# A four-level Perceiver on one core: the experts of levels 1 to 3 by one code on gathered tokens

## The chip, the cores and the metric

The kernel runs on one core of a Trainium2 chip. Its time is what the device measures for one execution, in microseconds (us); for the kernel before it is the median of three runs. The core has five engines with instruction streams of their own: TensorE (PE in the profile, PEld for its weight loads), VectorE (DVE), ScalarE (ACT), GpSimd (POOL) and SyncE (SP), which here only starts transfers. All arithmetic is float32; TensorE carries out each float32 matmul of the program as two instructions, so counts in the profile are twice those in the code.

## The reference, cut to what matters

A state x of 2 x 64 tokens (128 rows) with 256 features goes through four levels. Each level adds a cross-attention on a context (2 x 1024 x 192), a mixing stage, and a mixture of eight experts, each applied to the layer norm of x:

```python
x = x + _L1_attn_ref(_layernorm(x), L1_attn_W, L1_attn_b)
x = x + _L1_ffn_ref(_layernorm(x), L1_ffn_gate_w, L1_ffn_w1, L1_ffn_b1, L1_ffn_w2, L1_ffn_b2)
...
# _L1_ffn_ref                                   # 256 -> 1024 -> 256
logits = xf @ gate_w
top_w, top_idx = jax.lax.top_k(logits, 2)
top_w = jax.nn.softmax(top_w, axis=-1)
combine = jnp.zeros((t, 8)).at[jnp.arange(t)[:, None], top_idx].add(top_w)
h = jax.nn.gelu(jnp.einsum('td,edf->tef', xf, w1) + b1, approximate=False)
y = jnp.einsum('tef,efd->ted', h, w2) + b2
out = jnp.einsum('ted,te->td', y, combine)
# _L2_ffn_ref                                   # 256 -> 512 -> 256, no biases
h = jax.nn.silu(jnp.einsum('nd,ehd->neh', xf, w_gate)) * jnp.einsum('nd,ehd->neh', xf, w_up)
# _L3_ffn_ref                                   # 256 -> 1024 -> 256
gate_logits = x @ Wg + bg
h = jnp.einsum('td,edh->eth', xf, W0) + b0[:, None, :]
g = jax.nn.silu(jnp.einsum('td,edh->eth', xf, W1) + b1[:, None, :])
y = jnp.einsum('eth,ehd->etd', h * g, W2) + b2[:, None, :]
```

Each token uses its two best of the eight experts, so a quarter of all token-expert pairs counts. From the reference's routers, the tokens per expert are, for the inputs used: level 1: 57, 0, 41, 9, 7, 19, 51, 72; level 2: 34, 5, 16, 41, 1, 75, 42, 42; level 3: 0, 3, 26, 58, 109, 0, 54, 6.

## The kernel before, in words

The 128 tokens lie on the 128 partitions. The stages are called by level and place: l0x, l0a, l0f, l1x, l1a (a dynamic convolution), l1f, l2x, l2t (a test-time-trained layer with a Newton-Schulz iteration), l2f, l3x, l3a (a scan), l3f. In every stage TensorE multiplies, and ScalarE or VectorE takes the sums out of PSUM.

**Dense experts (l0f, l1f, l2f).** All 128 tokens go through all eight experts, one expert after the other, and the routing weight (zero for most) scales what comes out. `features` (L354) computes 128 hidden features at a time, with the weights as the stationary operand; `Mix.add` (L345) multiplies the hidden features by the second weights and adds the result, times the expert's column of `comb`, to x on VectorE (L349). `gate` (L301) is the router: it multiplies the transposed layer norm of x by the router's weights and finds the two best experts on VectorE. `expert_bias` (L328) adds l1f's second biases. `later` (L293) delays each expert's second matmuls behind the next expert's first. The first biases of l1f are added by ScalarE in its gelu (L1176), one activation for each 128 features.

**Gathered experts (l3f, from L1800).** A matmul with a triangle (`upto`, L1857) numbers the tokens of each expert; `to_slot` (L1865) is a one-hot matrix from tokens to 64 slots for each expert. A round r handles experts 2r and 2r+1 side by side, 64 columns each. `gather` (L1871) multiplies by the one-hot matrix, `hidden` (L1886) makes the hidden features with the tokens as stationary operand (64 columns) and the weights moving (512 wide), `turn` (L1905) transposes them, `out_of` (L1918) multiplies by the second weights, `scatter` (L1928) brings the rows back to their tokens and adds them to `acc` in PSUM. The bias sums start each PSUM bank by a matmul of one-hot rows (`biases`, L1822). After four rounds comes a fifth, OVER, of four blocks of 32 slots for experts with more than 64 tokens. Which experts these are is known only at run time: a chain on VectorE (L1948 to L1994) writes indices, and GpSimd fetches the blocks' weights by indirect transfers (L2011), twelve of 1 MB or as halves; a block that is not used has an index out of bounds, and nothing is moved for it.

**Buffers.** Weights go through a pool with three rings: w8 (six tiles of 1 MB), w4 (four tiles of 512 KB) and w2 (six of 256 KB). l3f has six more tiles of 1 MB (`more_w`). SyncE issues all other weight loads, in an order that a scheduler chose; each waits until the last reader of its buffer's previous content is done. `weight` (L124, transfer at L131) asks for a tile and starts its load.

**Order.** A scheduler orders the instructions of each engine, except in blocks under `in_written_order` (L268), where TensorE, VectorE, ScalarE and GpSimd keep the order of the code. Some work of later stages is written into earlier ones as filler (`steps`, L440): keys and values of l3x (L374 to L405) run in l1a, around l1f's end and around l2f.

`layernorm` (L225) takes statistics on VectorE, a square root on ScalarE with the activation table of the next function loaded behind it (`rstd_of`, L216), and a reciprocal; `transposed` (L240) transposes by TensorE and copies the result out of PSUM.

Of the kernel before, what the change touches and what calls it, by code (L numbers as in the profile page):

```python
# [17 lines left out]
P = 128  # L18
# [39 lines left out]
def tile_perceiver(ctx: ExitStack, tc: tile.TileContext, i: dict, out: bass.AP):  # L58
# [79 lines left out]
    routers = const.tile([P, 2, N_SMALL], F32, name="routers")  # L138
    ctx_gb = const.tile([CH, 4], F32, name="ctx_gb")
# [188 lines left out]
    def expert_bias(x, comb, b2):  # L328

        ps = bank()  # L330
        nc.tensor.transpose(ps[0:8, :P], comb, ident)
        cT = tok.tile([8, P], F32, tag="cT", name="cT")
        nc.vector.tensor_copy(cT, ps[0:8, :P])
        ps = bank()
        nc.tensor.matmul(ps[:, :D], cT, b2, start=True, stop=True)
        return residual(x, ps[:, :D])


# [101 lines left out]
    def steps(work, n=9):  # L440

        for _, _ in zip(range(n), work):
            pass

# [370 lines left out]
    steps(fill[0], 3)  # L815
    with psum(2, 4), stage_pool(name="l0a", bufs=1) as pool, in_written_order():
# [297 lines left out]


    with psum(2, 4), stage_pool(name="l1a", bufs=1) as pool, in_written_order():
# [24 lines left out]
        for k in range(6):  # L1141
# [8 lines left out]
            for r, dst in places:  # L1150
# [6 lines left out]
                )  # L1157
        bandT = transposed(band, 1, pool, "bandT", "bandT")
# [606 lines left out]
    with psum(2, 3), stage_pool(name="l3a", bufs=1) as pool:  # L1765
# [34 lines left out]
        x = residual(x, ps[:, :D])  # L1800

    with psum(2, 3), stage_pool(name="l3f", bufs=1) as pool, stage_pool(
# [230 lines left out]
        for r in range(OVER + 1):  # L2039
# [26 lines left out]
            if r:  # L2066
                out_of(r - 1, last_w2)
# [172 lines left out]
```

## Time and profile before

| what | us |
|---|---|
| median of three runs (741.34 to 745.24) | 742.32 |
| the profiled execution | 739.35 |
| its span, first to last instruction | 737.6 |
| TensorE busy | 673.0 |
| l1f: x of l1a done to x of l1f done | 211.04 to 277.69 |
| l2f: x of l2t done to x of l2f done | 536.34 to 583.18 |
| l3f: x of l3a done to x of l3f done | 646.88 to 734.80 |

The mean granted TensorE clock of the profiled execution is 0.972. In the profile, a line of the timeline gives a start, a length, the engine, the line of the code, the operation, what it writes and reads, the shapes and how many instructions stand together; brackets give idle time ahead of it and what ended it. The groups of instructions give busy time, then mean length in ns, then idle time ahead.

### The profile page before, as it was taken

Reading aid. Unit: us, or ns where it says so; the run is one execution under the profiler, and the core shown is the slowest. Engines: PE = TensorE matmul, PEld = TensorE weight load, DVE = VectorE, ACT = ScalarE, POOL = GpSimd, SP = SyncE. Lnnn points to the kernel's source line nnn. Section 1 sums busy time; section 2 is a strip of 40 time slices with the busy share of each in tenths; the row PEclk is TensorE's granted clock in tenths of the full one; section 3 lists DMA queues with packets and bytes.
Section 4 is the critical chain, followed back from the end, with each engine's and each line's share of the span. In section 5 each row is a group of like instructions: output and inputs, shape, how many; then the busy total and the mean of one; then the engine's idle time right before and its main releaser. Section 6 shows DMA issues by size and latency. Waiting matters only on the chain.

```text
span 737.6 us, 11286 instructions
## 1 busy us (share of the span) xinstructions
PE 673.0 (91%) x4624; PEld 497.3 (67%) x4624; DVE 284.7 (39%) x718; ACT 268.2 (36%) x542; POOL 66.6 (9%) x92
## 2 busy tenths in 40 slices
PE   7779979989879999999999989999999989679987
PEld 4446658856659996766767678999889756534434
DVE  5853443267440003343342344534232267451111
ACT  2352343278533333323333425306130388322111
POOL 3530100000100000000000030210000000000240
PEclk9999999999969999999999999999999999979999
DMA  9930013830006887000000400030158700628951
GB/s 292 422 141 1 15 36 119 304 120 2 1 1 232 289 294 270 1 0 1 1 1 9 163 1 1 1 109 7 59 199 289 254 0 2 267 94 347 419 192 73
DMA packets 19302, 92.76 MB, mean 126 GB/s; under 512 B 3298, under 2 KB 5876, under 8 KB 10068
## 3 DMA queue, kind: packets, MB, share of 16 engines
q1 hardware_dynamic: 16976, 85.70, 31.5%
q0 software_dynamic: 2016, 6.30, 2.3%
q8 instruction: 36, 0.59, 0.3%
q14 instruction: 14, 0.11, 0.0%
q10 hardware_dynamic: 260, 0.06, 0.0%
HBM read 98.20 MB, written 0.13 MB: 133 GB/s over the span
## 4 chain that ended last, share of the span: by engine, by line
PE 76%; DVE 8%; issue 7%; ACT 6%; DMA 2%; POOL 1%; POOLq 0%; DVEq 0%; ACTq 0%
PE bank L255 34%; PE two_banks L1245 4%; PE bank L988 4%; PE bank L247 3%; PE two_banks L959 3%; PE two_banks L1250 2%; PE bank L1014 2%; PE two_banks L1417 2%; PE two_banks L1896 2%; PE two_banks L374 2%; PE bank L1537 2%; PE two_banks L400 1%; ACT pT L997 1%; PE two_banks L255 1%; PE bank L1525 1%
## 5 line engine op out<-in xcount | busy, mean ns | idle before, releaser
L255 PEld LDWEIGHTS bank<-l2x_ctx,pT 128*128 128x128 f32 x256 | 42.2, 190 | 7.9 <-ACT pT L104 4.9
L255 PE MATMUL bank<-l2x_ctx,pT 128*128 128x192 f32 x256 | 44.4, 327 | 0.6 <-ACT pT L104 0.6
L349 DVE SCALAR_TENSOR_TENSOR x_new<-bank,comb,x_new 128x256 f32<-128x256 f32 x24 | 11.6, 483 | 80.0 <-PE bank L255 80.0
L988 PEld LDWEIGHTS bank<-ident,p 128*128 128x128 f32 x256 | 29.6, 149 | 17.3 <-issue 6.1
L988 PE MATMUL bank<-ident,p 128*128 128x128 f32 x256 | 39.4, 297 | 1.2 <-ACT pT L997 0.5
L967 DVE TENSOR_REDUCE negmax<-two_banks 128x1 f32<-128x1024 f32 x32 | 37.6, 1215 | 5.8 <-PE two_banks L959 5.8
L973 ACT ACTIVATE p<-two_banks,negmax 128x1024 f32<-128x1024 f32 x32 | 36.1, 1127 | 0.8 <-DVE negmax L967 0.8
L1245 PE MATMUL two_banks<-ctxA,l2x_qA 128*128 128x512 f32 x64 | 32.6, 597 | 0.5 <-DVE l2x_qA L102 0.5
L255 PEld LDWEIGHTS bank<-xT,l1f_w_sb 128*128 128x128 f32 x256 | 31.9, 204 | 0.6 <-issue 0.3
L255 PE MATMUL bank<-xT,l1f_w_sb 128*128 128x128 f32 x256 | 32.2, 287 | 0.0
L997 ACT COPY pT<-bank 128x512 f32<-128x512 f32 x48 | 26.9, 588 | 14.5 <-PE bank L988 14.5
L1176 ACT ACTIVATE l1f_hT<-bank,cols 128x128 f32<-128x128 f32 x64 | 18.3, 369 | 35.0 <-PE bank L255 35.0
L255 PEld LDWEIGHTS bank<-xT,l2f_w_sb 128*128 128x128 f32 x256 | 29.6, 192 | 0.3
L255 PE MATMUL bank<-xT,l2f_w_sb 128*128 128x128 f32 x256 | 29.8, 275 | 0.0
L104 ACT COPY pT<-bank 128x512 f32<-128x512 f32 (+1 forms) x22 | 12.1, 557 | 47.8 <-PE bank L247 47.8
L255 PE MATMUL bank<-l1f_w_sb,l1f_hT 128*128 128x256 f32 x128 | 28.8, 379 | 0.0
L1255 DVE TENSOR_REDUCE negmax<-two_banks 128x1 f32<-128x1024 f32 x16 | 19.6, 1224 | 20.8 <-PE two_banks L1250 20.8
L247 PEld LDWEIGHTS bank<-ident,p 128*128 128x128 f32 x164 | 17.7, 141 | 13.8 <-issue 11.8
L959 PE MATMUL two_banks<-n_kT,n_qx 32*128 32x512 f32 x128 | 23.8, 641 | 2.8 <-ACT n_kT L435 1.8
L255 PEld LDWEIGHTS bank<-l1f_w_sb,l1f_hT 128*128 128x128 f32 x128 | 23.8, 190 | 2.9
L262 POOL TENSOR_TENSOR x_bias<-x_new,rows 128x256 f32<-128x256 f32 x4 | 2.9, 726 | 240.7 <-DVE x_new L349 236.2
L247 PE MATMUL bank<-ident,p 128*128 128x128 f32 x164 | 22.6, 279 | 0.7 <-DVE pT L102 0.6
(552 smaller groups left out, 1318.9 us busy)
## 6 DMA issues: line engine op xcount, KB each, us to landing
l1f_w_sb<-in_l1f_w_dram SPq DMA_DIRECT2D x16, 1024.0 KB, 4.8
l3f_w_sb<-in_l3f_w_dram SPq DMA_DIRECT2D x12, 1024.0 KB, 5.1
more_w<-in_l3f_w_dram SPq DMA_DIRECT2D x12, 1024.0 KB, 9.7
l0f_w_sb<-in_l0f_w_dram SPq DMA_DIRECT2D x8, 1024.0 KB, 8.1
l2f_w_sb<-in_l2f_w_dram SPq DMA_DIRECT2D x8, 1024.0 KB, 4.7
l2f_w_sb<-in_l2f_w_dram SPq DMA_DIRECT2D x8, 512.0 KB, 4.6
xh<-in_ctx_dram SPq DMA_DIRECT2D x8, 192.0 KB, 5.2
l2x_ctx<-in_ctx_dram SPq DMA_DIRECT2D x1, 1536.0 KB
```

The lines of the kernel that those rows point to most:

```text
L247: nc.tensor.transpose(ps[:, c * P : (c + 1) * P], src[:, (at + c) * P : (at + c + 1) * P], ident)
L255: nc.tensor.matmul(dst, lhsT, rhs, start=(k == 0), stop=(k == len(pairs) - 1))
L374: nc.tensor.matmul(dst[n], ctxA[:, b, n, keys], w[:, 0, :], start=True, stop=False)
L959: nc.tensor.matmul(sc[u][:, n * 512 : (n + 1) * 512], qx[rows_, c, n, b].rearrange("p h q -> p (h q)"), kT[c, b][rows_, n, :], start=True, ...
L967: nc.vector.tensor_reduce(sc[u][1], sc[u][0], AX.X, ALU.max, negate=True)
L973: nc.scalar.activation(p[u], sc[u][0], AF.Exp, bias=sc[u][1], scale=1.0, accum_out=total[u // 4][:, u % 4 : u % 4 + 1],)
L988: nc.tensor.transpose(ps[:, kc * P : (kc + 1) * P], p[u][:, (4 * k + kc) * P : (4 * k + kc + 1) * P], ident,)
L997: nc.scalar.copy(dst, ps)
L1014: nc.tensor.matmul(po[32 * t : 32 * t + 32, :P], v[:, b, kc // 4, kc % 4, c * P + 32 * t : c * P + 32 * t + 32], pT[4 * g + t, k][:, kc % ...
L1176: nc.scalar.activation(hT[:, at + f, :], ps[:, f * P : (f + 1) * P], AF.Gelu, bias=col("l1f_b1", e * 8 + at + f), scale=1.0,)
L1245: nc.tensor.matmul(dst[n], qA[:, j, b].rearrange("p h q -> p (h q)"), ctxA[:, b, n, :], start=True, stop=False,)
L1255: nc.vector.tensor_reduce(negmax, sc, AX.X, ALU.max, negate=True)
```

## The change

l1f and l2f take the gathered form that l3f has, and all three call one function, `experts`. What a stage gives it: the kind ("gelu": one hidden matrix with bias; "gated": two halves of 512 columns, no bias; "both": two matrices with biases), its constants (`Counting`), where each weight tile lies (`Shelf`, with a function `place`), and the order in which GpSimd fetches the overflow's weights (`blocks`). l0f stays dense.

- **Router.** It reads the transpose of x itself. Since the layer norm is (x - mean) times rstd, the logits are (x W - mean * column sums of W) * rstd. The negative column sums, `less_sums`, are made once ahead of l0a by two matmuls with ones. In l1f and l2f rstd goes into the scale of the tanh; in l3f, with its bias, into one more VectorE operation. The layer norm is still computed, for the gather.
- **First biases.** `sums_of` writes the bias sums of round 0 in the stage in front: in l1a ahead of the transpose of the band, in l3a ahead of its last transposes.
- **Order inside a round.** The overflow's plan comes after round 0 on VectorE; `ways_back` (transposes of slot_w and comb, second biases) moved from round 0 to round 1.
- **Buffers.** l1f has four further 1 MB tiles. In l2f the second weights use w4 tiles, and in the overflow blocks 2 and 3 use halves in w2 tiles, each cleared by GpSimd ahead of its transfer. In l3f the overflow's order is now: first matrix of all blocks, second matrix (halves in w4 tiles for blocks 0 and 1), then the last matrix of blocks 2, 3, 0, 1. In the code n numbers a stage's matrices (1 and 0 give hidden features, 2 the output) and j the expert in a round, or the block of the overflow: n0 of j2 is block 2's second hidden matrix.
- **Else.** The l1f bias columns leave the constants; l1a, l1f and l2f use one PSUM bank fewer for single tiles.

The built program also differs, by the scheduler's choice, in l2x (both context matmuls of an iteration stand ahead of the weighing; before, one stood on either side), in some of l2t's order, and in where l3f's first bias matmuls stand: behind l3x's last matmuls, ahead of l3a's first transposes.

New functions, cut to what the prediction speaks of:

```python
class Shelf:
    def load(self, r):                    # by SyncE
        for n in self.order:
...
            for j in range(2):
                t = self.room(self.place(r, j, n), chunks * wide)
                nc.sync.dma_start(t, src[2 * r + j].rearrange("p c f -> p (c f)"))
...
    def fetch(self, blocks, index, index2):   # by GpSimd
        for j, n in blocks:
...
            tag = self.place(OVER, j, n)
            parts = 2 if tag == "halves" else 1
            for k in range(parts):
                size = chunks * wide // parts
                t = self.room(tag if parts == 1 else "w4" if size > 512 else "w2", size)
                if size == 512:
                    nc.gpsimd.memset(t, 0.0)
                at = index[:, j : j + 1] if parts == 1 else index2[:, j, k : k + 1]
                nc.gpsimd.indirect_dma_start(
...

def experts(name, kind, x, consts, shelf, blocks, pool, acc, bias=None, b2=None, fill=(), sums=None):
...
    steps(fill, 1)
    ps = bank()
    for c in range(2):
        nc.tensor.transpose(ps[:, c * P : (c + 1) * P], x[:, c * P : (c + 1) * P], ident)
    xT = tok.tile([P, 2, P], F32, tag="xT", name="xT")
    nc.scalar.copy(xT.rearrange("p c t -> p (c t)"), ps[:, :D])
    st, mv = stat(6, "bn_st"), stat(2, "bn_mv")
    nc.vector.bn_stats(st, x)
    nc.vector.bn_aggr(mv, st)
    r_ = rstd_of(mv[:, 1:2], 1, table)
    xl = tok.tile([P, D], F32, tag="xl", name="xl")
    nc.vector.tensor_scalar(xl, x, mv[:, 0:1], r_, ALU.subtract, ALU.mult)
    ps = bank()
    accumulate(ps[:, :8], [(xT[:, c, :], router(name, c)) for c in range(2)])
    steps(fill, 2)
...
    for r in range(OVER + 1):
        if r == OVER:
            sums = sums_of(kind, consts, own_over)
        elif r or sums is None:
            sums = sums_of(kind, consts, None if kind == "gated" else consts.of_pair[r])
        prod = hidden(r, sums)
        if r == 0:
            shelf.load(2)
            shelf.load(3)
        if kind != "gated":
            turn(r, prod, 0)
        if r:
            out_of(r - 1)
        if r < OVER:
            gather(r + 1)
        turn(r, prod, 0 if kind == "gated" else 1)
        if r == 0:
            plan_blocks()
        if r == 1:
            ways_back()
        if r:
            scatter(r - 1)
    out_of(OVER)
    scatter(OVER)
    return residual(x, acc)
```

The stages' own part of the diff, cut:

```diff
@@ -813,6 +1170,10 @@
     kv1.room(ahead1.enter_context(stage_pool(name="l1x_k", bufs=1)), pieces)
     fill = [kv1.keys(0, 0), kv1.keys(0, 1), kv1.keys(1, 0), kv1.values(1, 2)]
     steps(fill[0], 3)
+
+    ps = bank()
+    accumulate(ps[:, :N_SMALL], [(ones, routers[:, c, :]) for c in range(2)])
+    nc.scalar.mul(less_sums, ps[:, :N_SMALL], -1.0)
...
-
-    with psum(2, 4), stage_pool(name="l1a", bufs=1) as pool, in_written_order():
+    def place1(r, j, n):
+        if r == OVER:
+            return "more" if n == 1 else "w8"
+        return "more" if (r, n) in ((1, 2), (2, 1)) else "w8"
+
+    beside = ExitStack()
+    shelf = Shelf(
+        "l1f", (1, 2), place1, beside.enter_context(stage_pool(name="l1f_more", bufs=4))
+    )
...
@@ -1155,6 +1530,7 @@
                     dst, src[r, PAD - far : PAD - far + width], bits[r, k : k + 1], dst,
                     ALU.mult, ALU.add,
                 )
+        sums = sums_of("gelu", consts, consts.of_pair[0])
...
@@ -1163,25 +1539,15 @@
         steps(fill[2])
 
 
-    with psum(2, 4), stage_pool(name="l1f", bufs=2) as pool:
-        xlT = transposed(layernorm(x, then=AF.Gelu), 2)
-        mix = Mix(x, gate(xlT, "l1f"))
-        for e in range(8):
-            w1 = weight("l1f_w1", e)
-            w2 = weight("l1f_w2", e)
-            hT = pool.tile([P, 8, P], F32, name="l1f_hT")
-            for at in (0, 4):
-                ps = features(xlT, w1, at, 4)
-                for f in range(4):
-                    nc.scalar.activation(
-                        hT[:, at + f, :], ps[:, f * P : (f + 1) * P], AF.Gelu,
-                        bias=col("l1f_b1", e * 8 + at + f), scale=1.0,
-                    )
-            if e == 0:
-                mix.x = expert_bias(mix.x, mix.comb, l1f_b2)
-            later(lambda hT=hT, w2=w2, e=e: mix.add(hT, w2, e))
-        later()
-        x = mix.x
+    with psum(2, 3), stage_pool(name="l1f", bufs=1) as pool, stage_pool(
+        name="ps_acc", bufs=1, space=PSUM
+    ) as acc_pool, in_written_order():
+        x = experts(
+            "l1f", "gelu", x, consts, shelf,
+            [(j, n) for n in (1, 2) for j in range(4)],
+            pool, acc_pool.tile([P, D], F32, name="acc"), b2=l1f_b2, sums=sums,
+        )
+    beside.close()
 
 
...
@@ -1677,25 +2043,25 @@
 
 
     kv3.room(ahead.enter_context(stage_pool(name="l3x_k2", bufs=1)), [(0, 1), (1, 1)])
-    with psum(2, 4), stage_pool(name="l2f", bufs=2) as pool:
+    def place2(r, j, n):
+        if n == 1:
+            return "w8"
+        return "halves" if r == OVER and j >= 2 else "w4"
+
+    with psum(2, 3), stage_pool(name="l2f", bufs=1) as pool, stage_pool(
+        name="ps_acc", bufs=1, space=PSUM
+    ) as acc_pool:
+        shelf = Shelf("l2f", (1, 2), place2)
+        shelf.load(0)
...
+                "l2f", "gated", x, consts, shelf,
+                [(j, n) for n in (1, 2) for j in range(4)],
+                pool, acc_pool.tile([P, D], F32, name="acc"), fill=last,
+            )
 
 
...
+        def place3(r, j, n):
+            if r < OVER:
+                return "more" if r % 2 else "w8"
+            if n == 0:
+                return "halves" if j < 2 else "more"
+            return "w8" if n == 1 or j < 2 else "more"
...
+        sums = sums_of("both", consts, consts.of_pair[0])
         ps = bank()
         for c in range(2):
             nc.tensor.transpose(ps[:, c * P : (c + 1) * P], h[:, c, :], ident)
         x = residual(x, ps[:, :D])
...
+        x = experts(
+            "l3f", "both", x, consts, shelf,
+            [(j, 1) for j in range(4)] + [(j, 0) for j in range(4)]
+            + [(j, 2) for j in (2, 3, 0, 1)],
+            pool, acc_pool.tile([P, D], F32, name="acc"), row("l3f_bg"), l3f_b2,
+            sums=sums,
         )
```

More of the change, by code (lines that the diff above doesn't have):

```diff
@@ L1822, in biases @@
-        def biases(r):
-            psg, psh = two_banks(), two_banks()
-            mine = own_over if r == OVER else own_e[:, 2 * r : 2 * r + 2].rearrange(
-                "p e s -> p (e s)"
-            )
-            halves = [(ps, slice(k * 512, (k + 1) * 512)) for ps in (psg, psh) for k in range(2)]
-            for j, (ps, f) in enumerate(halves):
-                e = slice(32 * j, 32 * j + 8)
-                nc.tensor.matmul(
-                    ps[:, f], mine[e], bs[e], start=True, stop=False, skip_group_check=True
-                )
-            return psg, psh
@@ L1835, in tile_perceiver @@
-        xl = layernorm(x, then=AF.Silu)
-        xlT = transposed(xl, 2)
-        ps = bank()
-        accumulate(ps[:, :8], [(xlT[:, c, :], router("l3f", c)) for c in range(2)])
-        sums = biases(0)
-        lg, best = stat(8, "logits"), stat(8, "best")
-        nc.vector.tensor_tensor(lg, ps[:, :8], row("l3f_bg"), ALU.add)
-        nc.vector.max(best, lg)
-        at = small.tile([P, 8], U32, tag="at", name="at")
-        nc.vector.max_index(at, best, lg)
-        atf = stat(8, "atf")
-        nc.vector.tensor_copy(atf, at)
```

584 lines of the change are left out of this document (300 added, 284 removed), and 1 row of the table _COL.

## Prediction, on record before the result

> **What bounds the kernel now.** I read the busy shares and the chain of waits first, then a table of stretches around the three expert stages, then TensorE's and GpSimd's timelines inside them.
>
> ```profile
> PE 673.0 (91%) x4624; PEld 497.3 (67%) x4624; DVE 284.7 (39%) x718; ACT 268.2 (36%) x542; POOL 66.6 (9%) x92
> PE 76%; DVE 8%; issue 7%; ACT 6%; DMA 2%; POOL 1%; POOLq 0%; DVEq 0%; ACTq 0%
> ```
>
> TensorE is busy 91% of the span and carries 76% of the chain that ended last. So a time saved must be TensorE work removed or TensorE idle time closed. The table of stretches (span, then busy us of each engine with its instructions, granted clock, DMA share, GB/s):
>
> ```profile
> 211.00:217.20 6.20, 3.93 (x14) 2.14 (x13) 1.23 (x5) 3.05 (x5) 0.00 (x0) 0.50 0.00 0
> 217.20:277.70 60.50, 60.13 (x392) 56.08 (x392) 6.14 (x21) 19.78 (x66) 0.00 (x0) 0.96 0.73 252
> 536.30:540.00 3.70, 3.18 (x14) 1.19 (x13) 1.65 (x6) 2.91 (x5) 0.00 (x0) 1.00 0.46 193
> 540.00:583.20 43.20, 43.20 (x324) 41.22 (x324) 11.14 (x29) 6.28 (x11) 0.00 (x0) 1.00 0.75 267
> 646.90:656.20 9.30, 5.86 (x24) 3.60 (x24) 4.67 (x23) 2.70 (x6) 0.58 (x1) 0.58 0.27 111
> 656.20:734.80 78.60, 73.03 (x490) 34.24 (x490) 14.96 (x39) 12.65 (x25) 14.56 (x15) 0.96 0.62 241
> ```
>
> Rows 2 and 4 are the dense experts of l1f and l2f: TensorE is full, so fewer rows shorten them. Rows 1, 3 and 5 are the heads (router to first expert). l3f, which already gathers, has the long head: 9.30 us at clock 0.58. Row 6 has 5.6 us of idle time; it sits in the overflow block, on TensorE's timeline:
>
> ```profile
> 709.57 1.14 PE L1830 MATMUL two_banks<-l3f_bs,own_over 8*128 8x512 f32 x8
> 710.64 1.92 PE L1896 MATMUL two_banks<-over_t,l3f_xg 128*32 128x512 f32 x16
> 713.69 1.05 PE L1896 MATMUL two_banks<-over_t,l3f_xg 128*32 128x512 f32 x2 [1.13 <-DMA over_t<-in_l3f_w_dram,index]
> 717.29 1.06 PE L1896 MATMUL two_banks<-over_t,l3f_xg 128*32 128x512 f32 x1 [2.55 <-DMA over_t<-in_l3f_w_dram,index]
> ...
> 724.08 0.66 PE L1908 MATMUL bank<-ident,l3f_prod 128*128 128x128 f32 x4
> ```
>
> From 710.64 to 724.08 is 13.44 us for a step that takes 7.09 in an undisturbed round. It waits for two indirect DMAs that GpSimd issued only at 708.28 and 709.57.
>
> **Prices of the gathered form.** They come from l3f's third round:
>
> ```profile
> 681.87 1.14 PE L1830 MATMUL two_banks<-l3f_bs,own_e 8*128 8x512 f32 x8
> 682.95 7.09 PE L1896 MATMUL two_banks<-l3f_w_sb,l3f_xg 128*64 128x512 f32 x32
> 689.96 0.65 PE L1908 MATMUL bank<-ident,l3f_prod 128*128 128x128 f32 x4
> 690.55 3.67 PE L1922 MATMUL bank<-more_w,l3f_hT 128*64 128x256 f32 x32
> 694.15 0.71 PE L1875 MATMUL bank<-to_slot,xl 128*128 128x128 f32 x4
> ```
>
> The next round's hidden step starts at 696.74, so a round is 13.8 us. l1f has one hidden matrix instead of two: 16 of the 32 hidden instructions (3.55) and half the bias work (0.54) go: 13.8 - 3.5 - 0.5 = 9.8 per round. l2f has two halves of 512 columns, no bias, and half the out step (16 of 32, 1.83): 3.55 + 1.83 + gather 0.5 + turn 0.45 + scatter 0.52 = 6.85.
>
> **l1f.** Before: first expert at 217.21, last x_new done at 277.69. After: the transposes of x need no LayerNorm, but stand behind the filler (ends 213.45); the copy of xT stands on ScalarE behind n_v's (214.5) and ahead of the square root with its table load of 1.28, so logits come at about 217.3, as before (217.39). From logits to the first hidden step l3f takes 650.87 to 656.19 = 5.3, so hidden(0) starts at 222.7: 5.5 later than the first dense expert. It lasts 3.55, plus 1.2 for the cold clock (l3f's first hidden step takes 8.27 where a warm one takes 7.09). Turn and gather put hidden(1) at 229.9. Round 1 also holds the way back (slot_w's transposes, comb's, b2: about 2.2, from the 4.69 between hidden(0) and hidden(1) of l3f less 2.5 of turn, gather and bias): 12.0; rounds 2 and 3 take 9.8 each: hidden(4) at 261.5, its out step some 9 later, 3.67 long, ending at 273.9; scatter and residual add 1.7 (733.1 to 734.80 in l3f): x_new at 275.6. That is **-2.1**. The weights come in time: I followed each buffer to its last reader; the overflow's second matrix is issued after out_of(2) at about 259 and needs to be there by 270, where a 1 MB load takes 4.8 (5.3 if indirect: issued at 708.28, landed about 713.6). The bias sums moved into l1a run while TensorE idles there (205.9 to 208.5); pmod and own_e cost VectorE 0.84 between LayerNorm steps, mostly covered by ScalarE's table load up to 201.72: **+0.15**. The two matmuls of less_sums precede a TensorE wait of l0a: 0.
>
> **l2f, without waits.** Logits at about 539.9 (540.19 before), hidden(0) at 545.2, 5.2 later than the first dense expert (540.01). Then 3.55 + 1.2, hidden(1) at 551.45, a round 1 of 8.6 (6.85, the way back 0.9, and 0.8 since the plan's 4.95 us chain on VectorE delays m_prod), two rounds of 6.85: hidden(4) at 573.9, out_of(3) from 577.4 to 579.25, out_of(4) could start at 580.2 and x_new would come at 583.9 against 583.18: **+0.7**. Dense, the eight experts take 42.5; gathered 37.8, but behind a longer head.
>
> **l2f's new wait.** The overflow's out weights of blocks j2 and j3 are halves, and GpSimd issues them in order behind block j1's, whose w4 buffer is last read by out_of(3). Router counts of the inputs give l2f one overflow block, so j1 to j3 fetch nothing; but the wait and the issue stay. GpSimd's rows:
>
> ```profile
> 716.04 0.99 POOL L2011 DMA_INDIRECT over_t<-in_l3f_w_dram,index  x1 [0.30 <-issue]
> 717.33 0.99 POOL L2011 DMA_INDIRECT over_t<-in_l3f_w_dram,index  x1 [0.30 <-issue]
> ```
>
> An issue costs 0.99 plus a gap of 0.30, and these were empty (l3f has two blocks). Each half has a memset of 128x512 ahead (0.51, the row of qx). From 579.3: j1 0.99, then four times 0.51 + 0.30 + 0.99: the last issue starts at 586.5 and ends at 587.5. No row shows when an empty transfer reports. Bounds: at its issue's end (587.5), or as long as a real 1 MB (586.5 + 5.3 = 591.8). I take the smallest load with a landing, 55 KB in 2.6: 589.1. out_of(4) reads all four blocks in its first step, so TensorE idles from 580.2 to 589.1: **+8.9** (7.3 to 11.6). Nothing else can be done: the fillers are written behind it. It restarts cold, clock 0.58: 1.83 / 0.58, **+1.4** (0 to 2.5). l2f in all: +11.0.
>
> [...]
>
> **l3f.** n0's two blocks now go as halves into w4 tiles that are free, issued right behind n1 at about 694 to 698; they land by about 705 (saturated queues until 702), before hidden(4) needs them at 710. The 13.44 become 7.09: **-6.35**. n2 of j0 and j1 is issued about 707 to 710, lands 714 to 717.5, needed at 723. The biases of round 0 (650.77 to 652.86, which held the upto matmul by about 0.5) move to l3a, into an idle stretch at 637.84 to 640.01: **-0.4**. l3f: -6.8.
>
> **Elsewhere** the scheduler puts both context matmuls of l2x ahead of the weighing, and reorders some of l2t: same work, 0 (-1 to +1 each).
>
> **Sum:** 0.15 - 2.1 + 11.0 - 6.8 = +2.3 on the profiled execution's 739.35: 741.6; it lies 3 below the median, so on the median's level 742.32 + 2.3 = **744.6**. What a measurement can tell from no change is 0.5%, 3.7 us: faster is below 738.6, slower above 746.0.
>
> **Rivals.**
> - As forecast, with its bounds (l1f -3.5 to -0.5, the stall 7.3 to 11.6, l3f -7.2 to -5.5): 741 to 749. Chance 0.55: 0.02 faster, 0.33 same, 0.20 slower.
> - GpSimd's queue holds nobody (empty issues shorter, or the wait for out_of(3) not last): the 10.3 of stall and cold clock go: 734.3, faster. Against it: thirteen of the fourteen issue rows are 0.99, full and empty. Chance 0.15.
> - Slower by late weights: w4 has only three free slots in l2f (l3x_wk holds one), each refill waits for an out step and takes 4.6; it decides as soon as a round is shorter than out step to landing (6.85 against 4.6 + queueing behind 1 MB loads, 3.5). Two such waits and a cold clock after each, 3 to 4 each: 750 to 753. Chance 0.18.
> - l3f's gain fails: the halves, issued while SP's loads fill the queues (420 GB/s), land after 710, or POOL's order holds n2 late: up to +6.4: 751. Chance 0.12.
>
> Faster 0.17, same 0.33, slower 0.50. The range, 738 to 753, leaves out the first rival's 0.15 and a little above.
>
> **What would show it.** Right: TensorE idle some 9 us ahead of l2f's last out step, ended by a DMA of l2f's weights; l3f's hidden(4) at 7.1; l1f's last x_new about 64.5 us after l1a's; heads of 11 and 9 us. Wrong: waits on DMA inside rounds 1 to 3; hidden(4) of l3f still near 13; heads longer than 5.3 from logits to hidden(0), which would count three times.

## The result, and the profile after

The changed kernel takes **767.06 us** (median of four runs, 764.45 to 774.93) against 742.74 for the kernel before, measured beside it: a ratio of 1.0341, 95% interval 1.0255 to 1.0427. It is slower, as the forecast's sign said, but by 24 us and not by 2; the time lies outside the range (738 to 753). The profiled execution took 769.37 (span 767.5), 2.3 over its median, against 739.35 before, 3.4 under its own. The comparisons of stages below are made between these two, so they add up to 30 us where the medians lie 24 apart.

Two lines of the page after, in the order of the first two lines shown of before: busy time, then the chain that ended last.

```profile
PE 684.4 (89%) x4562; PEld 451.5 (59%) x4562; DVE 291.8 (38%) x768; ACT 265.4 (35%) x519; POOL 90.3 (12%) x122
PE 78%; DVE 8%; ACT 8%; issue 4%; DMA 1%; POOL 1%; ACTq 0%; POOLq 0%; DVEq 0%
```

TensorE has 62 instructions fewer and is busy 11.4 us longer. So the loss is not only idle time: fewer instructions take longer. The mean granted clock fell from 0.972 to 0.950. Summed over 2 us windows, the busy time at a lowered clock that a full clock would have saved is 28.1 us after and 16.6 before.

Stage by stage (from one x to the next, profiled executions; the last column is the best kernel of the experiments, e10):

| stage | before | forecast | after | e10 |
|---|---|---|---|---|
| l0x and l0a | 113.70 | 0 | 118.45 (+4.75) | 115.79 |
| l1f | 66.65 | -2.1 | 71.22 (+4.57) | 65.15 |
| l2x | 130.45 | 0 | 137.35 (+6.90) | 130.50 |
| l2t | 128.20 | 0 | 128.86 (+0.66) | 128.18 |
| l2f | 46.84 | +11.0 | 64.46 (+17.62) | 44.80 |
| l3f | 87.92 | -6.8 | 83.30 (-4.62) | 80.96 |
| the other five | 161.04 | +0.15 (l1a) | 161.12 (+0.08) | 162.77 |

The stretches that answer to those shown of before, with the same columns (span, busy us of TensorE, its weight loads, VectorE, ScalarE, GpSimd, granted clock, DMA share, GB/s): l1f's head and rest; l2f's head, rounds, and end; l3f's rest.

```profile
215.57:226.37 10.80, 6.23 (x22) 4.02 (x21) 4.03 (x21) 5.18 (x9) 0.59 (x1) 0.50 0.00 0
226.37:286.80 60.43, 55.36 (x381) 26.22 (x382) 7.81 (x30) 13.96 (x27) 8.61 (x9) 0.97 0.53 194
553.00:560.25 7.25, 4.53 (x22) 2.37 (x21) 4.22 (x23) 5.31 (x10) 0.08 (x1) 1.00 0.23 96
560.25:601.50 41.25, 36.88 (x209) 15.58 (x209) 10.55 (x33) 6.55 (x14) 7.33 (x8) 0.92 0.58 220
601.50:617.50 16.00, 6.91 (x36) 2.71 (x37) 0.42 (x1) 1.60 (x2) 6.08 (x8) 0.68 0.68 253
690.00:764.80 74.80, 73.04 (x490) 32.16 (x490) 14.63 (x40) 12.89 (x26) 14.45 (x15) 0.95 0.66 253
```

The heads (rows 1 and 3) are near their forecast of 11.7 and 8.86. Row 2 has 5 us of idle TensorE where the forecast had none, and row 5 has 9, at clock 0.68. In row 6 the idle time of l3f's overflow is gone (1.8 where before's row had 5.6).

**Where l1f's time went.** TensorE's timeline of round 2, up to the start of round 3, and then ScalarE's read of round 2's first half:

```profile
247.54 1.13 PE L551 MATMUL two_banks<-bs,own_e 8*128 8x512 f32 x4
248.60 1.94 PE L579 MATMUL two_banks<-more_w,m_xg 128*64 128x512 f32 x8
251.29 1.94 PE L579 MATMUL two_banks<-more_w,m_xg 128*64 128x512 f32 x8 [0.76 <-ACT m_prod L585]
259.92 1.94 PE L579 MATMUL two_banks<-l1f_w_sb,m_xg 128*64 128x512 f32 x8
```
```profile
250.64 0.60 ACT L585 ACTIVATE m_prod<-two_banks 128x512 f32<-128x512 f32 x1 [4.41 <-PE two_banks L579]
```

The hidden step is cut in two. TensorE fills the first 512 columns until 250.54; ScalarE reads them from 250.64 to 251.24; only then, at 251.29, does TensorE go on. The second half writes the other bank of the same two-bank tile, so nothing is overwritten; the program orders the write behind the read because it is one tile. The bias step shows 1.13 for four instructions where l3f's row has 1.14 for eight: half the biases cost the same. And 259.92 less 248.60 is a round of 11.3, not 9.8.

**Where l2f's time went.** The last out step on TensorE's timeline, and two of GpSimd's issues for it (block j1, and the first half of j3):

```profile
601.51 0.62 PE L627 MATMUL bank<-l2f_w_sb,m_hT 128*32 128x256 f32 x2 [0.17 <-DVE m_hT L618]
608.35 1.48 PE L627 MATMUL bank<-l2f_w_sb,m_hT 128*32 128x256 f32 x4 [6.22 <-DMA l2f_w_sb<-in_l2f_w_dram,index]
612.17 3.62 PE L627 MATMUL bank<-l2f_w_sb,m_hT 128*32 128x256 f32 x26 [2.35 <-DMA l2f_w_sb<-in_l2f_w_dram,index]
```
```profile
600.41 0.99 POOL L526 DMA_INDIRECT l2f_w_sb<-in_l2f_w_dram,index  x1 [6.96 <-PE bank L627]
605.85 1.00 POOL L526 DMA_INDIRECT l2f_w_sb<-in_l2f_w_dram,index  x1 [0.27 <-POOL l2f_w_sb L524]
```

This is the stall of the forecast: GpSimd waits for the out step of round 3, issues block j1 at 600.41, and then clears and issues the halves of j2 and j3. But TensorE resumes with j1's matrix at 608.35, 7.9 after its issue, and reaches j3's first half only at 612.17, 6.3 after its issue, though no weights are moved in either. The last row, 26 instructions in 3.62, runs at half clock (0.51 granted over it).

### The profile page after: what moved, and what is told of

Read it like the earlier page. It is cut to its first block, busy times and chain, and to the rows that moved or that the text cites. A ratio compares the mean times of both kernels' runs of the same rounds, so it can differ in the third digit from the quotient of the medians.

```text
span 767.5 us, 11269 instructions
## 1 busy us (share of the span) xinstructions
PE 684.4 (89%) x4562; PEld 451.5 (59%) x4562; DVE 291.8 (38%) x768; ACT 265.4 (35%) x519; POOL 90.3 (12%) x122
## 4 chain that ended last, share of the span: by engine, by line
PE 78%; DVE 8%; ACT 8%; issue 4%; DMA 1%; POOL 1%; ACTq 0%; POOLq 0%; DVEq 0%
PE bank L256 19%; PE two_banks L579 10%; PE bank L627 6%; PE two_banks L1611 4%; PE bank L1349 4%; PE two_banks L1616 3%; PE bank L248 3%; PE two_banks L1320 3%; PE bank L1375 2%; PE two_banks L1783 2%; PE two_banks L364 2%; PE bank L1903 2%; PE bank L612 2%; PE two_banks L390 1%; PE bank L598 1%
## 5 line engine op out<-in xcount | busy, mean ns | idle before, releaser
L590 DVE TENSOR_TENSOR m_prod<-two_banks,m_g 128x512 f32<-128x512 f32 x15 | 10.4, 691 | 59.0 <-PE two_banks L579 59.0
L618 DVE COPY m_hT<-bank 128x512 f32<-128x512 f32 x15 | 10.3, 690 | 57.0 <-PE bank L612 44.1
L1611 PE MATMUL two_banks<-ctxA,l2x_qA 128*128 128x512 f32 x64 | 30.3, 596 | 0.5 <-ACT l2x_qA L104 0.5
L104 ACT COPY pT<-bank 128x512 f32<-128x512 f32 (+1 forms) x22 | 12.1, 556 | 49.8 <-PE bank L248 49.8
L632 ACT COPY m_y<-bank 128x256 f32<-128x256 f32 x15 | 5.6, 372 | 64.0 <-PE bank L627 64.0
L579 PE MATMUL two_banks<-more_w,m_xg 128*64 128x512 f32 (+1 forms) x128 | 25.7, 597 | 1.5 <-ACT m_prod L585 1.5
L248 PEld LDWEIGHTS bank<-ident,p 128*128 128x128 f32 x164 | 17.8, 141 | 13.8 <-issue 6.5
L579 PE MATMUL two_banks<-l2f_w_sb,m_xg 128*64 128x512 f32 (+1 forms) x96 | 22.1, 664 | 4.0 <-ACT m_g L587 3.5
L579 PE MATMUL two_banks<-l3f_w_sb,m_xg 128*64 128x512 f32 (+1 forms) x112 | 25.0, 668 | 0.5 <-ACT m_xg L605 0.5
L587 ACT ACTIVATE m_g<-two_banks 128x512 f32<-128x512 f32 x15 | 9.0, 597 | 47.0 <-PE two_banks L579 47.0
L1616 PE MATMUL two_banks<-ctxB,l2x_qB 64*128 64x512 f32 x64 | 24.8, 641 | 0.0
L1634 DVE TENSOR_SCALAR l2x_u<-bank,rinv 128x192 f32<-128x192 f32 x16 | 6.7, 418 | 38.2 <-PE bank L256 38.2
```

What stands on the lines that cost most here:

```text
L248: nc.tensor.transpose(ps[:, c * P : (c + 1) * P], src[:, (at + c) * P : (at + c + 1) * P], ident)
L579: nc.tensor.matmul(part[s], xg[r][:, c, s], shelf.at[r, j, n](c, f), start=(kind == "gated" and c == 0), stop=(c == 1), skip_group_check=True,
L1611: nc.tensor.matmul(dst[n], qA[:, j, b].rearrange("p h q -> p (h q)"), ctxA[:, b, n, :], start=True, stop=False,)
L1616: nc.tensor.matmul(dst[n], qB[half[n], j, b].rearrange("p h q -> p (h q)"), ctxB[half[n], b, :], start=False, stop=True,)
```

## The experiments

The first four went to one chip, the next four to a second, the last four to a third, each set beside the kernel before (743.57, 742.47 and 744.17). "Below after" takes the median from 767.06; after ran beside 742.74, so a gap of one or two us between chips can hide in such a difference, and the ratios are what a conclusion rests on.

**e1: the halves of the hidden sums in tiles of their own.** After, with l1f's rounds from 1 on and all of l2f's:

```diff
-        parts = [(ps[:, low], 1, low, 0), (ps[:, high], 1, high, 1)]
+        second = two_banks()[:, low] if apart else ps[:, high]
+        parts = [(ps[:, low], 1, low, 0), (second, 1, high, 1)]
```

> The changed kernel with one edit: from round 1 on in l1f, and in every round of l2f, the two column halves of the hidden sums lie in two PSUM tiles instead of the two banks of one. Theory: TensorE's wait of 0.70 between the halves (for ScalarE to read the first half out of the same tile) goes, and the two runs of 1.94 become one of 3.55, so 4.6 becomes 3.6 in nine rounds: 9 us less than the changed kernel, 767 becomes 758. Rival: the wait is ScalarE's latency and only moves on to the transposes that read its result: 0 to 2 us less.

Measured: 760.36, ratio 1.0228 (1.016 to 1.0296); 6.7 below after. TensorE's row for the same round as above:

```profile
247.98 3.65 PE L580 MATMUL two_banks<-more_w,m_xg 128*64 128x512 f32 x16
```

One run of 16 instructions in 3.65 stands where two of 1.94 and a wait of 0.76 stood. l1f falls from 71.22 to 67.98, l2f from 64.46 to 58.28. The transposes behind it do not wait for ScalarE instead, so the wait was for the tile, not for ScalarE's work.

**e2: l2x's TensorE order written out as before had it.** After, with transposes, half-row pairs, weighing and values in before's order by hand.

> The changed kernel with l2x's TensorE instructions in the order that the kernel before had: the two half-row context matmuls (64 rows each, on different rows of the array) stay next to each other instead of having the value matmuls between them. Theory: such neighbours run at the same time and separated ones do not, which costs 1.05 seven times; l2x falls from 137.3 to 130.4, 6.9 us less. Rival: l2x is longer for another reason (later loads of its weights, other waits on the softmax): the order gives back under 1 us.

Measured: 768.18, ratio 1.035 (1.0267 to 1.0433): nothing gained in total, and l2x 135.40, not 130.45. Half of the reason held. In before's l2x the four instructions of the half-row context product (64 rows) stand together; in after they are split around the values in six iterations (below, before and then after):

```profile
315.29 1.13 PE L1250 MATMUL two_banks<-ctxB,l2x_qB 64*128 64x512 f32 x4
```
```profile
323.80 1.12 PE L1616 MATMUL two_banks<-ctxB,l2x_qB 64*128 64x512 f32 x2
324.85 0.66 PE L1651 MATMUL bank<-l2x_uT,l2x_wv_sb 96*64 96x128 f32 x8
325.44 1.12 PE L1616 MATMUL two_banks<-ctxB,l2x_qB 64*128 64x512 f32 x2
```

Side by side, four take 1.13; apart, two take 1.12. Such an iteration takes 8.26 instead of 7.21, and six times 1.05 is 6.3 of the 6.9 us of l2x. The written order put them together, but then a copy was late, ahead of every weighing: between 300 and 395 us TensorE's weight loads waited 13 times for VectorE's pT, 11.3 us in all, where in after the same wait came to 3.1. In both, VectorE makes that copy; in before, ScalarE did (L104). That led to e5.

**e3: the overflow's halves first.** After, with l2f's blocks 2 and 3 (the halves) fetched ahead of the rest, and blocks 0 and 1 in free w8 tiles, so that no issue waits for the out step of round 3:

```diff
-        return "halves" if r == OVER and j >= 2 else "w4"
+        if r == OVER:
+            return "halves" if j >= 2 else "w8"
+        return "w4"
...
-                [(j, n) for n in (1, 2) for j in range(4)],
+                [(2, 2), (3, 2)] + [(j, 1) for j in range(4)] + [(0, 2), (1, 2)],
```

> The changed kernel with other buffers and another order for l2f's overflow: the last matrix of blocks 2 and 3 (halves, tiles that are free) is fetched first, that of blocks 0 and 1 goes last into 1 MB tiles that hidden(3) frees, ten us ahead of its use. Theory: the last out step, 14.3 with its two waits (6.22 and 2.35) and the cold clock, becomes 1.9: 12.4 us less. Rival: an empty transfer reports late because SyncE's loads stand in the transfer engines, wherever it is issued: a wait of 2 to 5 stays, 7 to 10 us less.

Measured: 757.15, ratio 1.0169 (1.011 to 1.0229); 9.9 below after. The out step in one piece, at full clock (1.00), behind VectorE alone:

```profile
599.58 1.93 PE L627 MATMUL bank<-l2f_w_sb,m_hT 128*32 128x256 f32 x32 [0.17 <-DVE m_hT L618]
```

l2f falls by 13.4. What the others show of this stall: e7 and e9 below.

**e4: before, with only the new overflow order in l3f.** The halves (the branch under the first condition of each version) are now n0 of blocks 0 and 1, no longer n2 of blocks 2 and 3:

```diff
-            for m, n in enumerate((1, 0, 2)):
...
-                for k in range(4):
-                    if n == 2 and k >= 2:
...
+            order = [(1, k) for k in range(4)] + [(0, k) for k in range(4)]
+            for n, k in order + [(2, k) for k in (2, 3, 0, 1)]:
...
+                if n == 0 and k < 2:
...
+                if n == 1 or (n == 2 and k < 2):
```

> The kernel before with only l3f's overflow fetched in the changed kernel's order and buffers (second matrix of blocks 0 and 1 as halves, then blocks 2, 3, 0, 1 of the last). Theory: the fifth hidden step falls from 13.44 to 7.1 and nothing else is late: 6.3 us less than the kernel before, 742.5 becomes 736. Rival: the last matrix is now late and the wait moves to the last out step: 0 to 2 us less.

Measured: 736.64, ratio 0.991 (0.9877 to 0.9943): 6.9 gained, l3f from 87.92 to 82.19. This part of the change is worth about what the forecast gave it (-6.35).

**e5 and e6: which engine makes a copy.** Copies out of PSUM go through a function that alternates:

```python
    turn = [0]
    def evacuate(dst, src):
        turn[0] ^= 1
        if turn[0]:
            nc.vector.tensor_copy(dst, src)
        else:
            nc.scalar.copy(dst, src)
```

The count runs through the whole program. The gathered l1f and l2f have one such copy fewer each (the transpose of x is copied by ScalarE directly), so from l1f to l2f every copy changes its engine. e5 is after, with `turn[0] ^= 1` ahead of l2x and again ahead of l3x; e6 is before, with the same line ahead of l2x and ahead of l2f.

> The changed kernel with the toggle that hands PSUM copies alternately to VectorE and ScalarE flipped once ahead of l2x and once behind l2f; the change had removed one such copy in l1f and one in l2f, so between them every copy was on the other engine. Theory: that swap is why the scheduler chose another order in l2x, and it makes TensorE wait for the later copy of the softmax; with the flip the scheduler gives back the order of the kernel before in l2x and l2t, l2x falls from 137.35 to 130.45 and l2t from 128.9 to 128.2: 7.6 less than the changed kernel. Rival: the engines of the copies do not matter, only the order of TensorE, and the run with that order alone gave 135.4: 2 less.

> The kernel before with nothing but that toggle flipped ahead of l2x and flipped back ahead of l2f. Theory: l2x becomes 137.35 and l2t 128.9, as in the changed kernel, 7.6 more than before (742.7 becomes 750.3), with no expert touched. Rival: l2x's loss needs the changed kernel's later loads or its buffers: under 1 more.

Measured: e5 759.6, ratio 1.021 (1.0157 to 1.0264), 7.5 below after; l2x 130.50 and l2t 128.05, in TensorE's order of before. e6 750.78, ratio 1.0118 (1.0063 to 1.0174), 8.3 above before; l2x 137.29, in after's order. One line, put in at two places, takes the loss away or brings it into a kernel with nothing of the change in it.

**e7 and e9: what makes the empty transfers late.** e7 is after with e3's order of the blocks alone (tiles as in after, so one issue still waits for the out step). e9 is e7, with SyncE's six loads of 1 MB for l3f's first rounds put behind l3x's last weights.

> The changed kernel with l2f's overflow fetched in another order only: the four halves first, block 0's and 1's last matrix at the end, in the same tiles as in the changed kernel; block 1's transfer, which fetches nothing, is then the last thing that GpSimd issues, right behind out_of(3), at about 600.4, one us ahead of its use. If the stall was GpSimd's chain of clears and issues with a short landing (2.6, as I predicted), the wait falls from 8.6 to 1.5 to 2: 9 to 10 less. If an empty transfer itself takes as long as those of the changed kernel did (600.41 to 608.3, 605.85 to 612.1: 6 to 8), the first wait of 6.2 stays and only the second one of 2.35 goes: 2 to 4 less.

> The run with the halves first, and with l3f's six 1 MB loads ordered behind l3x's, so that SyncE starts only one load of 512 KB (l3x_wq, about 600.2) in the time in which block 1's empty transfer (issued about 600.4) is waited for; before, a 1 MB load started at 600.65 and two more at 592 to 598. Theory: an empty transfer is late because its descriptors stand in the same engines behind SyncE's megabytes; the wait of 5.6 falls to 1.5 to 2.5. Rival: an empty transfer takes 6 to 7 us by itself (its 128 rows are worked off all the same): 5 to 6 stays.

Measured, with two runs each: e7 762.86, ratio 1.0265 (1.0207 to 1.0323), l2f 60.25; e9 756.05, ratio 1.0162 (1.0122 to 1.0202), l2f 54.75. The out step that waits for the last issue in e7, and then that issue and the step in e9:

```profile
607.74 3.63 PE L627 MATMUL bank<-l2f_w_sb,m_hT 128*32 128x256 f32 x30 [5.59 <-DMA l2f_w_sb<-in_l2f_w_dram,index]
```
```profile
600.44 0.99 POOL L534 DMA_INDIRECT l2f_w_sb<-in_l2f_w_dram,index  x1 [6.96 <-PE bank L635]
...
603.96 1.93 PE L635 MATMUL bank<-l2f_w_sb,m_hT 128*32 128x256 f32 x30 [1.80 <-DMA l2f_w_sb<-in_l2f_w_dram,index]
```

In e7 one issue is left behind the wait, at 600.43, and TensorE still resumes 7.3 after it: GpSimd's chain of clears and issues, on which the forecast spent its working, is the smaller part. With SyncE's 1 MB loads out of the way it is 3.5 after. These are the loads that SyncE starts beside that issue, in e7 and then in e9:

```profile
600.23 0.33 SPq L131 DMA_DIRECT2D l3x_wq_sb<-in_l3x_wq_dram  x1
600.65 0.38 SPq L508 DMA_DIRECT2D l3f_w_sb<-in_l3f_w_dram  x1
```
```profile
600.24 0.33 SPq L131 DMA_DIRECT2D l3x_wq_sb<-in_l3x_wq_dram  x1
```

In e7 another of l3f's 1 MB loads went out just ahead of them, at 598.30. In after one went out at 598.27, and five follow between 600.21 and 602.15 (l3x_wq, two of l3a's, two of l3f's with 1 MB each). From 600 to 604 us the core's transfers move 375 and then 410 GB/s in e7, 94 and then 168 in e9. So an empty transfer reports later here where others move at the time: its reader goes on 7.3 us after the issue in e7, 3.5 in e9.

**e8: e1, e3 and e5 together**, and the copy of `less_sums` by VectorE instead of ScalarE.

> The changed kernel with four edits: two PSUM tiles for the halves, the toggle flipped back, l2f's overflow buffers and order of the earlier run, and the column sums copied out by VectorE instead of ScalarE, so that the table load of l0a's square root does not stand behind them. If the causes are independent, -6.7 - 7.6 - 9.9 - 0.7 on 767: about 742, as the kernel before; by the stages of the profiles (l1f 68.0, l2x 130.4, l2t 128.2, l2f 44.9, l3f 81.5 to 83) it is 733 to 737, 1% faster than before.

Measured: 742.66 (ten runs), ratio 1.0006 (0.9966 to 1.0045): no difference from before that can be told. Taken one at a time the three gave 6.7 + 9.9 + 7.5 = 24.1, and 767.06 less 24.1 is 742.96: they add up within what such medians can tell. The change's loss is accounted for, but the 733 to 737 that the stages of the profiles had promised did not come, though l2f has less work than before: its profile has l2f at 49.51 (before 46.84) where 44.9 was expected, and l3f at 84.29 for 81.5 to 83. The heads were tried next.

**e10: e8, with the square root first.** In the experts' head ScalarE copies xT, which comes late from TensorE, and behind it loads a table, takes the root and loads the next table:

```diff
-        xT = tok.tile([P, 2, P], F32, tag="xT", name="xT")
-        nc.scalar.copy(xT.rearrange("p c t -> p (c t)"), ps[:, :D])
         st, mv = stat(6, "bn_st"), stat(2, "bn_mv")
         nc.vector.bn_stats(st, x)
         nc.vector.bn_aggr(mv, st)
-        r_ = rstd_of(mv[:, 1:2], 1, table)
+        root, r_ = stat(1, "root"), stat(1, "rstd")
+        nc.scalar.activation(root, mv[:, 1:2], AF.Sqrt, bias=eps, scale=1.0)
+        xT = tok.tile([P, 2, P], F32, tag="xT", name="xT")
+        nc.scalar.copy(xT.rearrange("p c t -> p (c t)"), ps[:, :D])
+        table_for(table, root[:, 0:1])
+        nc.vector.reciprocal(r_, root)
```

> The run with all four edits, and in the three heads ScalarE takes the square root ahead of the copy of the transposed x (the next function's table behind the copy). Theory: the table load of 1.28 then runs while ScalarE has nothing to do, and the reciprocal, which the scaled tokens and l3f's logits need, is up to 1.3 earlier in each head: 2 to 4 less, 742.7 becomes 739 to 740. Rival: the copy of the transposed x, now behind the root, is what is late: 0 to 1 less or more.

Measured: **733.33** (732.05 to 735.2), ratio 0.9862 (0.9831 to 0.9893); 9.3 below e8 (whose ratio, on another chip, was 1.0006), where 2 to 4 were expected. ScalarE in l2f's head, after and then e10:

```profile
553.66 0.37 ACT L647 COPY xT<-bank 128x256 f32<-128x256 f32 x1 [2.30 <-PE bank L645]
554.05 1.28 ACT L220 ACT_TABLE_LOAD   x1
555.35 0.29 ACT L220 ACTIVATE root<-bn_mv,eps 128x1 f32<-128x1 f32 x1
```
```profile
538.96 0.29 ACT L651 ACTIVATE root<-bn_mv,eps 128x1 f32<-128x1 f32 x1 [1.06 <-DVE bn_mv L649]
539.16 0.35 ACT L653 COPY xT<-bank 128x256 f32<-128x256 f32 x1
```

One of two table loads in a row (1.28 each) is gone from between copy and root: it now stands ahead, in idle time. That is the 1.28 expected per head: from e8 to e10 the heads of l1f, l2f and l3f (from x to the first hidden step) fall from 10.80, 7.75 and 8.55 to 8.95, 6.39 and 7.54, 4.2 in all. The rest is the clock. TensorE's first hidden step of l2f, e8 and then e10:

```profile
548.36 6.03 PE L580 MATMUL two_banks<-l2f_w_sb,m_xg 128*64 128x512 f32 x16 [0.46 <-ACT m_xg L606]
```
```profile
544.63 3.65 PE L580 MATMUL two_banks<-l2f_w_sb,m_xg 128*64 128x512 f32 x16 [0.46 <-ACT m_xg L606]
```

The same 16 instructions take 6.03 behind the longer head and 3.65 behind the shorter. Between the profiles of e8 and e10, whose spans are 740.3 and 730.9, l1f, l2f and l3f gain 2.2, 4.7 and 3.3, and the busy time that the lowered clock costs falls from 25.3 to 19.7. That the shorter head brought the better clock is not shown by one profile of each: in l3f the first hidden step went the other way, from 9.06 to 9.50. The runs have mean clocks of 0.950 to 0.968 in e8 and of 0.962 to 0.970 in e10, and where they meet (0.965 to 0.968) those of e10 are still some 4 to 7 us shorter. This version is 1.4% faster than before.

**e11: before, with the column sums alone** (the two matmuls and ScalarE's copy of `less_sums`, which nothing reads). **e12: after, with l1f and l2f dense as before.**

> The kernel before plus the two matmuls of the column sums and ScalarE's operation that copies them out, ahead of l0a; nothing uses them. Theory: the table load of l0a's square root, which stood in idle time at 87.55, now waits behind that operation, so l0a is 0.66 longer, and the shift by this moves the stretches of half clock: l0a and l1x 23.4 and 53.2 become 25 to 26.3 and 54.3 as in most profiles of the changed kernel's family, 1 to 3.5 more in all. Rival: those two stages are longer for another reason of the change (PSUM split, buffers): 0.7 more and no other half-clock stretch.

> The changed kernel with l1f and l2f dense as before: what is left of the change is l3f in the common form (router on x itself, first biases in front, the overflow's new order) and the column sums. Theory: l3f 81 to 82, l3a 7.4 to 8.2, l0a 0.7 to 2.5 more, l2x and l2t as before since the toggle has its old phase: 736 to 738, about the run of the kernel before with l3f's order alone (736.6). Rival: the router on x itself and the biases in front are worth more than 1 us: below 735.

Measured: e11 744.81 (ten runs), ratio 1.0014 (0.9989 to 1.0038): nothing that can be told. e12 737.44, ratio 0.9913 (0.9888 to 0.9938), as e4's 0.991: the router on x itself and the biases written in front add nothing to the order of the transfers that these runs could tell. In e11's profile, though, the stages moved: l0a +2.8, l1f -2.3, l3f +2.4. In before the square root's table load of l0a starts at 87.55, ahead of its operation; in e11 it stands behind the copy of `less_sums` (90.66) and starts at 90.90 (in after 92.68 and 92.92). From there all is late by some 0.7, on top of 0.44 that l0x was longer, and the stretches of lowered clock fall elsewhere. In l0a, 105 to 114 us ran at full clock in before; 108 to 117 ran at 0.62 in e11. In the 17 us from l1a's end, over l1f's head and its first expert, it is the other way round, before and then e11 (the clock is the third figure from the end):

```profile
211.00:228.00 17.00, 14.36 (x82) 11.94 (x81) 3.51 (x18) 6.68 (x18) 0.00 (x0) 0.69 0.18 62
```
```profile
214.80:231.80 17.00, 14.15 (x91) 12.30 (x91) 3.47 (x18) 7.83 (x22) 0.00 (x0) 0.90 0.24 77
```

One is lost and the other gained, with an edit that does nothing later than l0a. That its 0.7 alone did this is not shown: the first half-clock stretch, long ahead of the edit, starts at 51.64 in e11 and at 51.04 in before, so the two executions differed already there.

## Why the prediction was wrong, step by step

The sign was right, but that is worth little: +2.3 was the small rest of larger terms, and less than the 3.7 that the forecast itself called no change. On the profiled executions it met +30.0. Of the 27.7 that it lacked, 7.56 lie in l2x and l2t, 6.67 in l1f, 6.62 in l2f, 4.75 in l0x and l0a and 2.18 in l3f. By its own terms:

- **l1f (-2.1, measured +4.57).** The head was 0.9 shorter than worked out. The step that failed is the price of a round, "13.8 - 3.5 - 0.5 = 9.8". l3f's hidden row is one run, because there the two matrices' sums lie in two tiles that take turns; the two halves of one tile follow each other only through ScalarE. A round took 11.3: 0.76 of wait, 0.3 more for two runs of 1.94 than for one of 3.55, and 0.5 for the bias work that was not halved in time. Round 0, whose first step ran at half clock (0.51 granted; eight instructions in 3.68, in round 2 in 1.94), took 8.8 where 7.2 was worked out. e1 shows the wait; that the bias matmuls share their time is read from the rows alone.
- **"Elsewhere" in l2x and l2t, "same work, 0 (-1 to +1 each)" (measured +7.6).** The step counted instructions, not what stands beside them: two half-row products cost one when they are neighbours (1.13 for the four instructions; apart, 1.12 for each two). The cause, the alternation of copies, was in no view of the profile before; it is in the code, and e5 and e6 show it from both sides.
- **l2f (+11.0, measured +17.62).** The stall's place and its cause were right. Mis-sized: from hidden(0) to hidden(4) 33.45 where 28.7 was worked out (the wait inside hidden again, and clock 0.92), +4.8; from there to where the last out step could start, 7.8 for 6.3; the stall with its out step 14.28 for 12.13 (1.83 / 0.58 adds 1.3, not the 1.4 of the sum). The stall's term failed in "the smallest load with a landing, 55 KB in 2.6": the empty ones took 6.3 to 7.9. The upper bound, 5.3 of a real 1 MB, was passed too; e7 and e9 put that down to the transfers beside it. That TensorE's idle time itself, 6.22 and 2.35, came to 8.6 for the 8.9 forecast is luck: part of the step ran between the two waits, and what it last waited for was j3's first half, issued 1.8 ahead of the half that the sum had counted to. The head was 1.6 shorter than forecast.
- On the same point: from the start of the issue to the reader the runs have 3.5 with one load of 512 KB beside it (e9; 2.5 from the issue's end) and 7.9 beside five and more (after). No run here has an empty transfer alone, so what it takes by itself is not shown.
- **l3f (-6.8, measured -4.62).** Right in its mechanism: the overflow's hidden step takes 7.0 where it took 13.44, and e4 has the gain by itself (-5.7 in l3f, -6.9 in all). What is missing in after is clock: the third round's hidden step took 8.78 at a lowered clock (0.81), where a round of before had 7.09, and the first took 9.15 for 8.27. In after, the third round's hidden step, and then the overflow's from its start to the transposes behind it:

```profile
717.64 8.78 PE L579 MATMUL two_banks<-l3f_w_sb,m_xg 128*64 128x512 f32 x32
...
747.03 2.34 PE L579 MATMUL two_banks<-l3f_w_sb,m_xg 128*32 128x512 f32 x18
...
754.04 0.66 PE L612 MATMUL bank<-ident,m_prod 128*128 128x128 f32 x4
```

- **l0a (0, measured +2.3).** "The two matmuls of less_sums precede a TensorE wait of l0a: 0" overlooked ScalarE: the copy holds up a table load (from 87.55 in before to 90.90 in e11). Its own price is 0.7; the rest is clock, and over ten runs e11 is not longer than before by an amount that can be told. l0x's +2.46 is not of the change: with l0x's code alike, profiles have between 90.23 (e6) and 94.00 (e12), and the longer ones have more half-clock stretches on the way (one in before, from 51.04; two in after, from 52.50 and 76.39; three in e12). The forecast's +0.15 was for l1a, which came out 0.20 shorter.
- **The rivals.** "GpSimd's queue holds nobody" fell with after's stall, and e3, which took the wait ahead of that queue away, gained 9.9. "Late weights" inside the rounds did not come: what TensorE waited for in l2f's hidden steps was m_g, and in l1f's m_prod, both reads by ScalarE. "l3f's gain fails" fell with e4. None of them held the two largest surprises, the tile and the alternation.

What stays open is why the clock is lowered in one head and not in another (in before, 0.50 in l1f's and 1.00 in l2f's). One half of the answer is in the traces. Read in windows of 0.2 us (before and after) or 2 us (the experiments), the half-clock stretches of each profile (0.50 granted), but for one that the program's end cuts off, are whole multiples of 3.41 us long, from one (3.4) to five (17.1, around l1f's head in after, from 212.92), and within one profile all of them start on one grid of that step. In before they start at 51.04, 156.85, 208.05, 593.76, 641.54, 648.37 and 716.64, which lie 31, 15, 113, 14, 2 and 20 steps apart. In after the grid lies elsewhere (first start 52.50). Whether the grid follows the program is not shown: before, e4 and e6 have their first start at 51.04, 51.04 and 50.96.

The other half, what comes ahead of a step at half clock, the traces do not show. TensorE's busy share alone does not settle it: in after a step of 3.41 us that was 85% busy (from 72.98) was followed by one at 0.50, and one that was 53% busy (from 42.26) by one at 1.00. So none of these runs tells beforehand which head will run at a lowered clock.

## What to carry to other kernels

A step priced from another stage's row keeps that price only with that stage's neighbours, tiles and clock: ask of each row what stood beside it, and whether one tile or two lay under it. A transfer that moves nothing is not free (3.5 to 7.9 us from issue to reader here), and what releases it can release larger ones beside it (after, e7); where data may be absent, place those transfers in buffers that are free early (e3: -9.9). In a short chain between dense stages, the order on ScalarE decides whether a table load is hidden (e10: 4.2 in three heads). The -9.3 of e10 holds more clock than that; whether a shorter idle stretch brings it is not shown.

## What the runs showed of the hardware

- Two matmuls on 64 rows each (four instructions) ran side by side as neighbours in the order, in 1.13; with the value matmuls between them they took 1.12 each. Bias matmuls on 8 rows show the like: four instructions take 1.13, eight take 1.14.
- The empty indirect transfer of l2f's block j1 lets its reader go on 3.5 us after its issue in e9, 7.3 in e7 and 7.9 in after. From 600 to 602 and from 602 to 604 us the core's transfers move 94 and 168 GB/s in e9, 375 and 410 in e7, 363 and 315 in after.
- The lowered clock costs 16.6 us of TensorE's busy time in before, 28.1 in after and 19.7 in e10. In every profile it comes at 0.50 granted, in whole steps of 3.41 us on one grid (but for a stretch that the program's end cuts off), whose place differs between profiles (first start 51.04 in before, 51.64 in e11, 52.50 in after). So one stage of two profiles can differ by up to 3.8 us without a cause of its own (l0x, 90.23 to 94.00 with the same code).
